# Two graph layers on one core: adjacency and mask of the graph two ahead are loaded at another place in the DMA queue

## The chip, the cores and the metric

The kernel runs on one core of a Trainium2 chip. The metric is the device time of one execution in microseconds, the median of the runs; a profiled execution of the same kernel gives the trace that is read here. The engines are named as the profile names them: PE is TensorE (PEld its weight loads), DVE is VectorE, ACT is ScalarE, POOL is GpSimd and SP is SyncE. In this kernel SyncE computes nothing: it issues nearly all DMA transfers, in the order of its program.

## The reference

64 graphs of 256 nodes with 512 features pass through two layers, in float32. Layer 0 is graph attention with 8 heads over the adjacency matrix; layer 1 is attention with 8 heads of 64 whose weights get two more terms, from the adjacency and from exp(-distance), where both the adjacency and the distance are the same matrix `adj`. Each layer ends with a residual and a layer norm. Cut to what matters:

```
# layer 0
feats = einsum('bnf,hfu->bhnu', X, W)
dense = leaky_relu(e_self[..., :, None] + e_neigh[..., None, :], 0.2)
dense = dense + NEG_BIG * (1.0 - A[:, None, :, :])
out = einsum('bhij,bhju->bhiu', softmax(dense), feats) + b
x = layernorm(x + relu(out))
# layer 1
q, k, v = split(x @ W_qkv)
attn = softmax(where(mask, q @ k.T * scale, -big)) * LA
attn = attn + LG * adj + LD * exp(-dist)          # dist is adj
x = layernorm(x + (attn @ v) @ W_out + b_out)
```

## The kernel before

One graph of 256 nodes is a block; a tile has 128 partitions, so a block has two row tiles. The work on a block is cut into stages: `turned` and `proj0` (features of layer 0, by Strassen-like products of halves), `attend0` (attention of layer 0), `proj1` (q, k and v of layer 1), `softmax1` and `attend1` (attention and output of layer 1). The main loop runs over the block number b from 2 to 63. Each pass is made of two functions written out by hand: `attention0_beside_projections1(b)` and then `attention1_beside_projections0(b)`. They interleave steps of several blocks: attention 0 of block b, projections of block b-1 for layer 1, features of block b+1, softmax of block b-1, output of block b-2 and the store of block b-4. `second_beside_first()` is the fill: it does the same for the first blocks, before the loop.

The order is that of the source. After each step, `in_order()` ties every new instruction to the one before it on the same engine, so that no scheduler moves it. What an engine does next is thus what the source names next for it, and a DMA that has to wait holds back all later DMAs of SyncE.

The order of SyncE's transfers in a pass, with their lines, is this. First half: the store of the output of block b-4 (`out_dram<-y`, L1216), the reload of rows for a residual (`y<-hs`, L1092), the rows of x for layer 0's residual of block b (`x<-in_x_dram`, `load_rows`, L147), the blocked x of block b+2 (`xb`, four DMAs, L123), the rows after layer 0 to memory and back in blocks (`hs<-x`, L899, and `hb<-hs`, four DMAs, L123). Second half: the maximum of the row factors (`gs<-top`, L586), the row factors to memory (`gs<-grow_sb`, four DMAs, L597) and back to all partitions (`gb<-gs`, 1,028 KB, L601); then the inverted sums of the softmax to memory (`rs<-rec`, L1038) and back to all partitions (`rb<-rs`, 1,024 KB, L1039); then the adjacency and the mask of block b+2 (`load_adj`, four DMAs of 64 KB, L123, and one of 32 KB, L143).

The buffers around them: `adj` has one buffer, which is read by one transposition on VectorE (`aT`, L739, shown as L130 in the trace) in the first half of each pass, before the load in its second half; `mask` has four; `y` has one, so `y<-hs` waits until the store before it has landed; the rows of x share one buffer with the blocks `hb`, which are transposed (`hT`) in the second half.

The readers that the text names: L823 (`attend0`, step `end`) adds the rows of x to layer 0's output on VectorE; L670 (`columns`) reads the broadcast row factors gb; L1059 (`attend1`, `weights`) reads the broadcast sums rb; L351 is VectorE's addition after a product, L790 the matmuls of layer 0's attention, L87 the matmuls of all projections.

Of the kernel before, what the change touches and what calls it, by code (L numbers as in the profile page):

```python
# [17 lines left out]
def kernel(  # L18
# [31 lines left out]
    NB, N, F = x.shape  # L50
# [43 lines left out]
    def in_order():  # L94

        new = []
        for ins in reversed(nc.cur_bb.bb.instructions):
            if ins.name in traced:
                break
            traced.add(ins.name)  # L100
            new.append(ins)
        for ins in reversed(new):
            if ins.engine in last:
                tc.add_manual_dep(
                    ins,
                    last[ins.engine],
                    mybir.DependencyInfo(
                        mybir.DependencyClass.NoSync, mybir.DependencyReason.DATA
                    ),
                    reason="order of the source",  # L110
                )
            last[ins.engine] = ins.name
# [7 lines left out]
    def load_blocks(dst, src):  # L120

        for q in range(Q):
            nc.sync.dma_start(  # L123
                dst[q * B : (q + 1) * B],
                src.rearrange("(k r) (c q s) -> q r c k s", r=B, q=Q, s=B)[q],
            )
# [7 lines left out]
    def load(b):  # L134

        XB[b] = io.tile([P, C, N // B, B], FT, tag="xb", name=f"xb_{b}", bufs=1)
        load_blocks(XB[b], x[b])

    def load_adj(b):
        ADJB[b] = io.tile([P, T, N // B, B], FT, tag="adj", name=f"adj_{b}", bufs=1)  # L140
        load_blocks(ADJB[b], adj[b])
        MROW[b] = io.tile([P, N], U8, tag="mask", name=f"mask_{b}", bufs=4)
        nc.sync.dma_start(MROW[b], nodemask[b].partition_broadcast(P))  # L143
# [105 lines left out]
    def load_rowmask():  # L249
        for g in range(NB // B):  # L250
            for k in range(Q):
                nc.sync.dma_start(
                    rowmask[k * B : (k + 1) * B, g].rearrange("p i b -> p (i b)"),
                    maskz[g * B : (g + 1) * B, :],
                )

    def load_wo():

        wo12 = work.tile([P, C2, F2], FT, tag="p", name="wo12", bufs=5)
        parts = w_out.rearrange("(k c p) (g f) -> k g p c f", k=2, p=P, g=2)  # L260
        for dst, k, g in ((wo_sb[0], 0, 0), (wo12, 0, 1), (wo_sb[1], 1, 0), (wo_sb[2], 1, 1)):
            nc.sync.dma_start(dst, parts[k, g])
        return wo12
# [976 lines left out]
    def do(stage, b, step, *args):  # L1240

        if 0 <= b < NB:
            if (stage, b) not in S:
                S[stage, b] = stages[stage](b)
            S[stage, b][step](*args)
            in_order()
# [133 lines left out]
    def second_beside_first():  # L1380


        b = 1
        for g in range(2):
            for t in range(T):
                do("attend0", b, "product", g, t)
        CW[0](3)
        do("attend0", b, "rec0", 0)
        do("attend0", b, "rec0", 1)
        do("proj1", 0, "qk", "p3")  # L1390
        load_rowmask()
        nc.sync.dma_start(bo_bc, b_out.partition_broadcast(P))
        WO["12"] = load_wo()
        do("turned", 2, "xT")
        do("proj1", 0, "qk_add", 12)
        do("turned", 2, "xC")
        do("attend0", b, "norm0", 0, 0)
        do("proj1", 0, "values", "p1")
        do("attend0", b, "norm0", 0, 1)
        do("attend0", b, "norm0", 1, 0)  # L1400
        do("proj1", 0, "values", "p2")
        do("proj1", 0, "v_add", 11)
        do("proj1", 0, "values", "p6")
        do("attend0", b, "norm0", 1, 1)
        do("attend0", b, "end")
        right_factors(wf_sb, wf12, (1, 2))
        do("proj1", 0, "values", "p5")
        do("proj1", 0, "values", "p7")
        do("proj1", 0, "v_add", 22)
        right_factors(wf_sb, wf12, (3,))  # L1410
        load(3)
        do("proj0", 2, "product", "p1")
        do("proj1", 0, "values", "p4")
        do("attend0", b, "squares", slice(0, 1), False)
        do("proj0", 2, "product", "p6")
        do("attend0", b, "squares", slice(1, 2), slice(0, 2))
        do("proj1", 0, "values", "p3")
        do("proj0", b, "shared")
        do("proj0", 2, "aT")
        do("proj1", 0, "v_add", 12)  # L1420
        do("proj0", 2, "product", "p5")
        do("proj0", 2, "product", "p7")
        do("attend0", b, "norm")
        do("proj1", b, "blocks")
        do("proj0", 2, "add", 22)
        do("proj0", 2, "product", "p2")
        do("proj0", 2, "product", "p4")
        do("proj0", 2, "far")
        do("proj0", 2, "product", "p3")
        right_factors(wo_sb, WO["12"], (0, 1))  # L1430
        do("proj0", 2, "add", 11)
        do("proj0", 2, "add", 12)
        do("proj0", 2, "rows")
        do("proj1", b, "from_rows", 0)
        do("proj1", b, "from_rows", 1)
        do("proj0", 2, "shared", 0)
        do("softmax1", 0, "scores", 0)
        do("proj0", 2, "shift")
        do("proj0", 2, "broadcast", 0)
        do("softmax1", 0, "scores", 1)  # L1440
        do("proj0", 2, "shared", 1)
        do("proj0", 2, "bias")
        do("proj0", 2, "broadcast", 1)
        do("proj0", 2, "shared", 2)
        do("proj1", b, "hC")
        do("softmax1", 0, "both", 0)
        do("softmax1", 0, "scores", 2)
        do("softmax1", 0, "both", 1)
        do("softmax1", 0, "scores", 3)
        do("softmax1", 0, "both", 2)  # L1450
        do("softmax1", 0, "both", 3)
        do("proj1", b, "qk", "p1")
        do("proj1", b, "qk", "p2")
        do("softmax1", 0, "sums")
        do("softmax1", 0, "invert")
        do("proj0", 2, "columns")
        do("softmax1", 0, "inverted")
        load_adj(3)

    def attention0_beside_projections1(b):  # L1460

# [83 lines left out]
    def attention1_beside_projections0(b):  # L1545


        do("attend1", b - 2, "values", 0)
        do("attend1", b - 2, "values", 1)
        do("proj0", b + 1, "rows")  # L1550
        do("proj0", b + 1, "shared", 0)
        do("attend1", b - 2, "values", 2)
        do("attend1", b - 2, "values", 3)
        do("softmax1", b - 1, "scores", 0)
        do("proj0", b + 1, "shared", 1)
        do("proj0", b + 1, "shift")
        do("proj0", b + 1, "shared", 2)
        do("proj0", b + 1, "broadcast", 0)
        if b + 2 < NB:
            do("turned", b + 2, "xT")  # L1560
        do("softmax1", b - 1, "scores", 1)
        do("attend1", b - 2, "half_blocks", 0)
        do("proj0", b + 1, "broadcast", 1)
        do("softmax1", b - 1, "both", 0)
        do("attend1", b - 2, "half_blocks", 1)
        do("softmax1", b - 1, "scores", 2, 0)
        do("softmax1", b - 1, "scores", 2, 2)
        do("softmax1", b - 1, "both", 1)
        do("softmax1", b - 1, "scores", 3, 0)
        do("attend1", b - 2, "product", "p1")  # L1570
        do("softmax1", b - 1, "scores", 2, 3)
        do("softmax1", b - 1, "scores", 3, 1)
        do("softmax1", b - 1, "both", 2)
        do("proj1", b, "hT")
        do("softmax1", b - 1, "both", 3)
        do("attend1", b - 2, "product", "p2")
        do("attend1", b - 2, "product_add", 11)
        do("attend1", b - 2, "product", "p6")
        do("attend1", b - 2, "product", "p5")
        do("attend1", b - 2, "product", "p7")  # L1580
        do("attend1", b - 2, "product_add", 22)
        do("softmax1", b - 1, "sums")
        do("proj1", b, "hC", (0,))
        do("softmax1", b - 1, "invert", 0)
        do("proj1", b, "hC", (2,))
        do("softmax1", b - 1, "invert", 1)
        do("proj1", b, "hC", (1,))
        do("softmax1", b - 1, "invert", 2)
        do("proj1", b, "hC", (3,))
        do("attend1", b - 2, "product", "p4")  # L1590
        do("proj0", b + 1, "bias")
        do("softmax1", b - 1, "inverted")
        if b + 2 < NB:
            load_adj(b + 2)
        do("attend1", b - 2, "product", "p3")
        do("attend1", b - 2, "product_add", 12)

# [126 lines left out]
```

## Time and profile before

| | us |
|---|---|
| median of 3 runs | 2842.19 (2837.35 to 2842.84) |
| the profiled execution | 2837.97 |
| its span, first to last instruction | 2835.8 |
| TensorE busy | 2791.4 (98%) |
| VectorE busy | 2561.0 (90%) |
| ScalarE busy | 1797.0 (63%) |
| DMA queue of SyncE, share of 16 DMA engines | 46.9% |

The granted TensorE clock was 0.998. TensorE is busy in nearly every slice of the span, so the time is read from the gaps: for a stall of TensorE, who released it, and for that one, what it had waited for. The longest waits of all engines stand at the top of the list of waits, but most belong to engines with time to spare:

```profile
POOL rstd_l L402 <- ACT junk L391: 1010.8, 129, 17.6
POOL nmean_l L385 <- DVE x L823: 996.1, 64, 28.0
```

In such a line the engine, its instruction and the releaser are followed by the total in microseconds, the number of waits and the longest. GpSimd is 15% busy, and its waits are idle time. The lines of the order of time begin with the start and the length in microseconds; SyncE's lengths are those of the issue, not of the transfer, and "x4" stands for four instructions in a row.

### The profile page before, as it was taken

Reading aid. Unit: us, or ns where it says so; the run is one execution under the profiler, and the core shown is the slowest. Engines: PE = TensorE matmul, PEld = TensorE weight load, DVE = VectorE, ACT = ScalarE, POOL = GpSimd, SP = SyncE. Lnnn points to the kernel's source line nnn. Section 1 sums busy time; section 2 is a strip of 40 time slices with the busy share of each in tenths; the row PEclk is TensorE's granted clock in tenths of the full one; section 3 lists DMA queues with packets and bytes.
Section 4 is the critical chain, followed back from the end, with each engine's and each line's share of the span. In section 5 each row is a group of like instructions: output and inputs, shape, how many; then the busy total and the mean of one; then the engine's idle time right before and its main releaser. Section 6 shows DMA issues by size and latency. Waiting matters only on the chain.

```text
span 2835.8 us, 93561 instructions
## 1 busy us (share of the span) xinstructions
PE 2791.4 (98%) x38584; PEld 2240.6 (79%) x38584; DVE 2561.0 (90%) x5264; ACT 1797.0 (63%) x5051; POOL 426.6 (15%) x1031
## 2 busy tenths in 40 slices
PE   9999999999999999999999999999999999999998
PEld 7778778788788787877777878887777878878775
DVE  7899999999989899899999999999998989999884
ACT  4666666666666666666666666666666666666663
POOL 1111211111111111111111111111111111111111
PEclk9999999999999999999999999999999999999999
DMA  6444544444454445444444454454544444444432
GB/s 140 117 114 134 133 126 137 127 131 141 118 137 136 111 138 135 125 137 118 129 137 124 135 138 120 137 131 124 143 118 129 129 125 137 131 130 138 118 118 72
DMA packets 778390, 362.58 MB, mean 128 GB/s; under 512 B 694767, under 2 KB 696303, under 8 KB 761966
## 3 DMA queue, kind: packets, MB, share of 16 engines
q1 hardware_dynamic: 775854, 356.07, 46.9%
q8 instruction: 306, 5.01, 0.7%
q14 instruction: 118, 0.97, 0.1%
q10 hardware_dynamic: 2112, 0.52, 0.1%
HBM read 288.11 MB, written 68.13 MB: 126 GB/s over the span
## 4 chain that ended last, share of the span: by engine, by line
PE 90%; DVE 4%; DMA 3%; ACT 2%; issue 1%; POOL 0%; SPq 0%; DVEq 0%; POOLq 0%
PE pq_p L87 26%; PE po_p L87 14%; PE pf_p L87 12%; PE pv_p L87 12%; PE pz L951 8%; PE av L1078 8%; PE av L790 7%; PE pd L988 2%; DMA x<-in_x_dram 1%; DMA out_dram<-y 1%; ACT v L725 1%; DVE p L1059 1%; DVE y L1097 1%; DVE p L1068 1%; PE po L87 0%
## 5 line engine op out<-in xcount | busy, mean ns | idle before, releaser
L87 PE MATMUL pq_p<-hC,wqk_sb 128*64 128x128 f32 x8192 | 474.3, 273 | 11.1 <-issue 9.5
L87 PEld LDWEIGHTS pq_p<-hC,wqk_sb 128*64 128x64 f32 x8192 | 450.5, 137 | 14.8 <-issue 12.0
L767 DVE SCALAR_TENSOR_TENSOR pT<-gb,ccol,at 128x256 f32<-128x256 f32 x992 | 403.0, 477 | 17.2 <-ACT ccol L677 17.2
L87 PE MATMUL pq_p<-hT,wqk_sb 128*64 128x128 f32 x6144 | 360.3, 273 | 0.6 <-issue 0.5
L972 ACT ACTIVATE p<-pz,hide 128x512 f32<-128x512 f32 x638 | 337.6, 619 | 30.4 <-PE pz L951 30.4
L87 PEld LDWEIGHTS pq_p<-hT,wqk_sb 128*64 128x64 f32 x6144 | 343.9, 137 | 11.1 <-issue 2.2
L1059 DVE TENSOR_TENSOR p<-p,rb 128x1024 f32<-128x1024 f32 x252 | 298.8, 1206 | 3.7 <-DMA rb<-rs 3.7
L1068 DVE TENSOR_TENSOR p<-p,ct 128x1024 f32<-128x1024 f32 x252 | 299.3, 1208 | 0.2
L811 ACT ACTIVATE x<-av,rec 128x64 f32<-128x64 f32 x1024 | 223.9, 334 | 62.2 <-DVE rec L803 62.2
L790 PE MATMUL av<-v,pT 128*64 128x65 f32 x8192 | 253.5, 222 | 5.6 <-issue 4.9
L87 PE MATMUL pf_p<-wf_sb,xC 128*64 128x264 f32 x1984 | 257.4, 387 | 1.1
L87 PE MATMUL pv_p<-wv_sb,hC 128*64 128x256 f32 x2048 | 247.2, 380 | 11.0 <-DVE v L351 8.6
L348 ACT COPY qk<-pq_p 128x512 f32<-128x512 f32 x256 | 148.8, 581 | 171.2 <-PE pq_p L87 168.2
L790 PEld LDWEIGHTS av<-v,pT 128*64 128x64 f32 x8192 | 249.5, 138 | 8.0 <-issue 6.8
L725 ACT ACTIVATE v<-v 128x64 f32<-128x64 f32 x1024 | 251.2, 336 | 3.8 <-DVE v L716 3.7
L348 ACT COPY v<-pv_p 128x256 f32<-128x256 f32 x256 | 95.4, 373 | 226.6 <-PE pv_p L87 226.5
L951 PE MATMUL pz<-qk 64*128 64x256 f32 x2048 | 238.7, 383 | 0.0
L87 PE MATMUL po_p<-wo_sb,oC 128*64 128x256 f32 x1984 | 237.6, 381 | 0.5
L1078 PE MATMUL av<-p,v 128*64 128x256 f32 x2016 | 230.1, 379 | 2.1 <-DVE p L1068 2.1
L402 POOL TENSOR_SCALAR rstd_l<-rstd_l 128x2 f32<-128x2 f32 (+1 forms) x130 | 76.5, 589 | 1010.9 <-ACT junk L391 1010.8
L951 PEld LDWEIGHTS pz<-qk 64*128 64x128 f32 x2048 | 192.5, 187 | 44.8 <-issue 24.8
L87 PEld LDWEIGHTS pv_p<-wv_sb,hC 128*64 128x64 f32 x2048 | 162.3, 137 | 73.9 <-DVE v L351 13.3
(175 smaller groups left out, 4631.1 us busy)
## 6 DMA issues: line engine op xcount, KB each, us to landing
rb<-rs SPq DMA_DIRECT2D x63, 1024.0 KB
gb<-gs SPq DMA_DIRECT2D x62, 1028.0 KB
hs<-x SPq DMA_DIRECT2D x64, 512.0 KB
xb<-in_x_dram SPq DMA_DIRECT2D x252, 128.0 KB
x<-in_x_dram SPq DMA_DIRECT2D x63, 512.0 KB
y<-hs SPq DMA_DIRECT2D x63, 512.0 KB
out_dram<-y SPq DMA_DIRECT2D x63, 512.0 KB
hb<-hs SPq DMA_DIRECT2D x248, 128.0 KB
```

The lines of the kernel that those rows point to most:

```text
L87: matmul(dst[cols], lhsT[:, cols], rhs, **flags)
L348: nc.scalar.copy(out[COPIES[p]], dst)
L402: nc.gpsimd.tensor_scalar(rstd, rstd, 1.0 / F, EPS, op0=ALU.mult, op1=ALU.add)
L725: nc.scalar.activation(v[:, :U], v[:, :U], AF.Copy, scale=v[:, U : U + 1])
L767: nc.vector.scalar_tensor_tensor(pT[h][:, j, :], GB[b][h], CCOL[b][:, j, h : h + 1], AT[b][:, j, :], op0=ALU.max, op1=ALU.mult,)
L790: matmul(av[r * half : (r + 1) * half, k, :], pT[h][:, j, i : i + half], V0[b][:, j, h, :UA], start=(j == 0), stop=(j == T - 1),)
L811: nc.scalar.activation(X1[b][:, t, h * U : (h + 1) * U], av[:, k, :U], AF.Copy, scale=REC0[g][:, t, k : k + 1],)
L951: matmul(pz[r][:, j, :], QK[b][rows, g, 1, j * P : (j + 1) * P], QK[b][rows, g, 0, :], start=True, stop=True,)
L972: nc.scalar.activation(to, of, AF.Exp, bias=hide[:, j, b : b + 1], scale=U**-0.5)
L1059: nc.vector.tensor_mul(p, p, REC[b][:, k : k + 2, g // 2, :] .unsqueeze(2) .to_broadcast([P, 2, T, N]),)
L1068: nc.vector.tensor_add(p, p, CT[b].unsqueeze(1).to_broadcast([P, 2, T, N]))
L1078: matmul(av[0][r * U : (r + 1) * U, g % 2, :], V1[b][:, j, 2 * g + r, :], PROBS[b][g][:, r, j, :], start=(j == 0), stop=(j == T - 1),)
```

## The change

`load_adj(b + 2)` is called at another place of the same function: right behind the step that issues the broadcast of the row factors (gb), and no longer behind the step that issues the broadcast of the inverted sums (rb). In the fill, `load_adj(3)` is called right behind the transposition that reads the only `adj` buffer (`aT` of block 2), and no longer at the end of the function. `load_adj` itself and all other steps stay as they are.

```
@@ in second_beside_first
         do("proj0", b, "shared")
         do("proj0", 2, "aT")
+        load_adj(3)
         do("proj1", 0, "v_add", 12)
...
         do("softmax1", 0, "inverted")
-        load_adj(3)
@@ in attention1_beside_projections0
         do("attend1", b - 2, "half_blocks", 0)
         do("proj0", b + 1, "broadcast", 1)
+        if b + 2 < NB:
+            load_adj(b + 2)
         do("softmax1", b - 1, "both", 0)
...
         do("softmax1", b - 1, "inverted")
-        if b + 2 < NB:
-            load_adj(b + 2)
         do("attend1", b - 2, "product", "p3")
```

In the program as built, the order of the instructions of TensorE, VectorE, ScalarE and GpSimd is the same before and after; on SyncE's queue the five DMAs of `load_adj` stand ahead of `rs<-rec` instead of behind `rb<-rs`, and in the fill ahead of `hs<-x` of block 1.

More of the change, by code (lines that the diff above doesn't have):

```diff
@@ L1419, in second_beside_first @@
         do("proj0", 2, "aT")
+        load_adj(3)
         do("proj1", 0, "v_add", 12)
@@ L1457, in second_beside_first @@
         do("softmax1", 0, "inverted")
-        load_adj(3)
     def attention0_beside_projections1(b):
@@ L1563, in attention1_beside_projections0 @@
         do("proj0", b + 1, "broadcast", 1)
+        if b + 2 < NB:
+            load_adj(b + 2)
         do("softmax1", b - 1, "both", 0)
@@ L1592, in attention1_beside_projections0 @@
         do("softmax1", b - 1, "inverted")
-        if b + 2 < NB:
-            load_adj(b + 2)
         do("attend1", b - 2, "product", "p3")
```

## The prediction

> **What bounds the kernel now.** I read the page first, then the waits of TensorE, VectorE and SyncE's queue, then the order of time on SyncE in one bad block and in the last block.
>
> ```profile
> PE 2791.4 (98%) x38584; PEld 2240.6 (79%) x38584; DVE 2561.0 (90%) x5264; ACT 1797.0 (63%) x5051; POOL 426.6 (15%) x1031
> ...
> q8 instruction: 306, 5.01, 0.7%
> ```
>
> TensorE is busy for 98% of the span, so a change of DMA order can only win what TensorE stands still. The loop shows how much that is. The broadcast of the sums (rb<-rs, L1039) is issued once a block, at 131.66 us for the first full block and at 2736.54 us for the last: 60 blocks of 43.41 us. Blocks without a stall repeat every 42.66 us or so. So 60 x 0.75 = 45 us are stalls; that is the whole stake, plus little in the fill. What are they?
>
> ```profile
> PE pq_p L87 <- issue: 10.0, 10, 2.0
> PE pv_p L87 <- DVE v L351: 8.6, 10, 1.8
> PE av L790 <- issue: 4.9, 4, 2.4
> ```
>
> Two kinds (columns: total us, times, longest). First, TensorE waits for v, which VectorE adds late because it stood before L823, the residual of layer 0, for rows of x:
>
> ```profile
> DVE x L823 <- DMA x<-in_x_dram: 21.1, 16, 3.9
> ...
> DVE x L823 <- issue: 16.6, 17, 2.7
> ```
>
> (12.9 us more are booked under ACT, 8 times; all are the same instruction, and I read them all as the x load.) Second, "issue": TensorE waits for nothing that the program asked for. In every one of these the last packet of queue q8 (16,384 bytes, TensorE's instructions) began 2.2 to 2.4 us before TensorE went on. So these are late instruction fetches.
>
> A bad block on SyncE, then the instruction on VectorE that pays:
>
> ```profile
> 1162.93 0.35 SPq L601 DMA_DIRECT2D gb<-gs  x1
> 1170.05 0.56 SPq L1038 DMA_DIRECT2D rs<-rec  x1
> 1171.78 0.35 SPq L1039 DMA_DIRECT2D rb<-rs  x1
> 1172.18 2.83 SPq L123 DMA_DIRECT2D adj<-in_adj_dram  x4
> 1175.05 1.90 SPq L143 DMA_DIRECT2D mask<-in_nodemask_dram  x1
> 1177.05 0.39 SPq L1216 DMA_DIRECT2D out_dram<-y  x1
> 1182.64 0.37 SPq L1092 DMA_DIRECT2D y<-hs  x1
> 1183.05 0.47 SPq L147 DMA_DIRECT2D x<-in_x_dram  x1
> ```
>
> ```profile
> 1189.76 0.69 DVE L823 SCALAR_TENSOR_TENSOR x<-x,x 128x512 f32<-128x512 f32 x1 [3.87 <-DMA x<-in_x_dram]
> ```
>
> Adjacency and mask keep SyncE for 4.8 us ahead of the store; y<-hs cannot be issued before the store has landed, and x stands behind it. The last block loads no adjacency anywhere:
>
> ```profile
> 2736.54 0.35 SPq L1039 DMA_DIRECT2D rb<-rs  x1
> 2740.14 0.39 SPq L1216 DMA_DIRECT2D out_dram<-y  x1
> 2743.44 0.38 SPq L1092 DMA_DIRECT2D y<-hs  x1
> 2743.86 0.47 SPq L147 DMA_DIRECT2D x<-in_x_dram  x1
> ```
>
> Counted from rb, the store goes out at 3.60, where it waits for ScalarE's normalisation and no longer for SyncE; x goes out at 7.3, against 9 to 12.4 in the others. Its packets end at 12.6, and L823 starts at 14.0 without a wait. And where adjacency is to go, SyncE idles:
>
> ```profile
> SPq L1038 <- DVE nd L670: 418.5, 60, 7.3
> SPq L1092 <- DMA out_dram<-y: 224.1, 61, 5.2
> ```
>
> Behind gb it waits 418.5 / 60 = 7.0 us for rec before rs<-rec.
>
> [...] the 128-byte packets of adjacency begin at 1175, just as the 8,192-byte packets of rb run out, and the store's 2,048-byte packets follow at 1178. [...] 5.01 MB / 306 = 16.4 KB, and 78,401 TensorE records / 306 = 256. [...]
>
> **The change part by part.** Nothing is added: the loop moves five DMAs a block (4 x 64 KB and 32 KB) on SyncE's queue from behind rb to behind gb. TensorE, VectorE, ScalarE and GpSimd keep their order. The moved DMAs pass rs<-rec and rb<-rs, nothing else. Their buffers are free: adj was read by the transposition (L739) in the first half of the same block, and there are four masks.
>
> The new place. gb is issued 8.8 us before rb (6.8 to 9.1). Four issues at 0.63 to 0.8 us are 2.8 us. The mask's issue took 1.9 us more [...], and ended 4.3 to 7.6 us after rb's issue, typically 4.8; gb is as large as rb, so I take 4.8 behind gb: done at -4.0, and rs<-rec goes at -1.73. The packets: gb moved from 1164 to 1168, the DMA engines then idled until 1171.6. Adjacency's 2,048 packets of 13 ns are 1.7 us over 16 engines, 2.2 us as seen; it would end at about -1.4, the mask's few packets at -1. rs<-rec may be held up to 0.5 us by them. I take 0.2. The store has 3.2 us of slack on SyncE behind rb, and rb's reader (L1059 at +8.9) over 3 us after the landing: nothing.
>
> The old place, x rows. The store goes out at 3.6 instead of 4.4 to 7.7; x moves by at least 1.2 us, most where it was latest. How a wait at L823 counts: 3.87 us made a block of 45.50, 2.19 of 43.82, 0.98 of 43.10, under 0.5 of 42.7. So roughly the first microsecond is hidden by TensorE's lead. Over the blocks whose stall is this one, the excess over 42.67 sums to 23 us. I shifted each block's landing by what its store is late of 3.6, plus 0.5 us for adjacency's packets ahead of it: one wait stays above 1 us (the block at 1171, 1.7 us). Removed: 21 of 23. If cover is lacking elsewhere (slow landing), the same waits come back at most as before.
>
> The old place, instruction fetch. Twelve blocks with an "issue" stall carry 21 us over 42.67. The fetches fell due 3.9 to 6.3 us after rb, were served at 7.4 to 11.5, behind rb, adjacency and store in turn, and TensorE's densest stretch (the av products, 70 instructions a microsecond at +5 to +9) ran dry. Without adjacency the store's packets end at about 6.7 instead of 8.5 to 9. A fetch due at 4.2 is needed by about 6.3; served at 6.6, it costs 0.3 instead of 2.4. From below: nothing is gained, as the y and x loads (7.5 to 12.5) now block instead. From above: 19. I take 12.
>
> The new place, fetch. Transfers now fill -7.8 to -1 without a gap. A fetch due at -8 is served by -1.4, its instructions are needed at about +0.7, less 2.3 us of latency: up to 0.4 us late. One block in six has a fetch due in the critical 2 us. Bounds 0 and 10 us; I take 2.
>
> The fill. The one load moved waits for the transposition at 71.4 and is issued from 71.5 to 74.6; hs<-x at 73.20 goes 1.5 us later, with no reader for blocks; gs<-top (76.57) and gb (82.14) keep their times. Behind rb at 91 the av products lose their 6.3 us (3.3 in the loop) to a late fetch; some of it goes. Bounds 0 and 4; I take 2.
>
> Sum: 21 + 12 - 2 + 2 = 33. The profiled execution took 2837.97 us (span 2835.8 and 2.2 around it), so 2805. The median of the runs is 4.2 us higher; I take that for more stalls of the same two kinds, half of which would go: 2807.
>
> **The rivals.** (1) Fetch stalls only move: x waits go, but the fetches find the y and x loads or gb with adjacency. For: the packets of y and x start 2 us earlier, into the dense stretch; the last block, without adjacency, still shows a fetch due at 7.3 served at 9.9. Against: after +9 TensorE needs 40, then 18 instructions a microsecond, so such fetches have time. 2842 - 21 = 2821. (2) x does not come earlier: the store is held by ScalarE (SyncE waited for it 56 times, 28.8 us) and by its landing behind rb. Against: the last block. Then 2842, no change. (3) Slower: adjacency's issues hold SyncE behind gb until after rec is ready. rs, rb, store, y and x all follow in one queue. It decides where rb comes over 1.3 us later than now, as x then lands later than before; the mask's issue would have to take 8.5 us instead of 4.8. At 2.5 us every block's x is 1.2 us later than today, about 1.1 us a block beyond the hidden part: 66 - 23 - 12 = 31 slower, 2873. For: the mask's issue did take 7.6 us in one block, and gb is only 5 us ahead of rs in two. Against: 7.0 us of idle SyncE in 60 blocks.
>
> **How the numbers follow.** Forecast 0.62 (2796 to 2815 for itself), rival 1 0.20 (2815 to 2834), rival 2 0.07, rival 3 0.11. About 0.2%, 5.7 us, is what a measurement of this kernel tells from no change. Faster: 0.62 + 0.20, less a little of rival 1's edge, 0.81; within 0.2%: 0.08; slower: 0.11. The range 2796 to 2836 leaves out rivals 2 and 3.
>
> **What would show it.** Right: x issued 7.3 to 8 us after rb; the L823 waits at 50 us in all fall under 15; TensorE's "issue" waits under 8 us; the SyncE wait at L1038 falls to 2 us. Wrong: rb's distance from gb grows beyond 9 us; TensorE's "issue" waits keep 16 us or turn up around rb's issue; L1216 is not held by ScalarE.

## The result

The changed kernel takes 2797.98 us (median of 4 runs, 2796.61 to 2799.13) against 2839.81 us (2837.35 to 2842.84; median of 4, one run more than in the table of before): a ratio of 0.9852, with a 95% interval of 0.9835 to 0.9869. That is 41.8 us less. The profiled execution took 2798.83 us, 39.1 us less than the one before, with a span of 2796.9 us. The forecast was 2807 us. The direction held, and so did the two terms that it was made of; the profiled gain was almost 20% larger than forecast (39 us against 33), and one of the terms was much too small.

The page of the changed kernel, the line of engine busy times:

```profile
PE 2778.1 (99%) x38584; PEld 2201.3 (79%) x38584; DVE 2561.5 (92%) x5264; ACT 1794.7 (64%) x5051; POOL 417.0 (15%) x1031
```

The 38,584 matmuls are the same, and still TensorE's busy time is 13 us shorter than the 2791.4 us before. The granted clock is 0.998 in both. Of the 39 us, 26 are idle time that went and 13 are busy time that went, so a part of the stalls must have been booked as busy: a busy share of 98% hid more standing than 2%.

TensorE's waits of the changed kernel, from the list of waits (total us, times, longest):

```profile
PE pv_p L87 <- ACT v L348: 3.4, 3, 2.4
PE av L1078 <- DVE p L1068: 2.1, 2, 1.6
PE pq_p L87 <- ACT qk L348: 1.5, 3, 0.7
PE av L790 <- issue: 1.1, 4, 0.4
```

Both kinds of stall are nearly gone. "Issue" was 16.3 us in three groups before (10.0 and 4.9, and 1.4 under pv_p) and is now 1.4 (this line and 0.3 under pq_p); the wait of pv_p for VectorE's v, 8.6 us before, is no longer in the list. The first line was there before with the same 3.4 us.

The reason on VectorE, what ended the idle time ahead of L823 in the changed kernel:

```profile
  ACT v L348: 1.9, 1
  ACT x L811: 0.8, 2
  DMA x<-in_x_dram: 0.8, 2
  issue: 0.4, 1
```

That is 3.9 us in 6 waits, against 51.4 us in 43 before (21.1, 16.6, 12.9 and 0.8). On SyncE, one block in order of time, near the place of the bad block of before:

```profile
1147.81 0.35 SPq L601 DMA_DIRECT2D gb<-gs  x1
1148.21 2.62 SPq L123 DMA_DIRECT2D adj<-in_adj_dram  x4
1150.87 2.80 SPq L143 DMA_DIRECT2D mask<-in_nodemask_dram  x1
1154.99 0.55 SPq L1038 DMA_DIRECT2D rs<-rec  x1
1156.71 0.31 SPq L1039 DMA_DIRECT2D rb<-rs  x1
1160.32 0.39 SPq L1216 DMA_DIRECT2D out_dram<-y  x1
1163.16 0.37 SPq L1092 DMA_DIRECT2D y<-hs  x1
1163.58 1.23 SPq L147 DMA_DIRECT2D x<-in_x_dram  x1
```

Adjacency and mask now fill SyncE's wait for rec, and rs<-rec is still issued 7.2 us behind gb. The store goes out 3.61 us behind rb (5.27 in the block of before) and x 6.87 us behind it (11.27). SyncE's waits of the changed kernel say it for all blocks, and below them stands the line of before that the prediction only quotes:

```profile
SPq L1216 <- ACT v L725: 202.8, 60, 3.5
...
SPq L1092 <- DMA out_dram<-y: 187.4, 61, 5.3
...
SPq L1038 <- DVE nd L670: 106.1, 60, 6.2
```

```profile
SPq L1216 <- ACT v L725: 28.8, 56, 3.5
```

SyncE waits for rec 1.8 us a block instead of 7.0, and for ScalarE's normalisation ahead of the store 3.4 us instead of 0.5. The list names L725, but what ends there is the normalisation of y just ahead of it on ScalarE; in the block above:

```profile
1158.78 1.52 ACT L410 ACTIVATE y<-y,shift_l,rstd_l 128x512 f32<-128x512 f32 x2
```

It ends at 1160.30 us, and the store is issued at 1160.32. ScalarE, no longer SyncE, sets when the store goes. From rb of the first full block (130.56 us) to that of the last (2696.10) are now 60 blocks of 42.76 us, 0.65 us less each, 39 us in all: the whole gain lies in the loop. 42.69 us is the most frequent distance, so about 4 us of stalls are left there.

That distance is also the most frequent one before, so each block's excess over it can be put down to its stall (a block with both kinds is counted under "issue"). Before, 14 blocks with an issue stall carry 24 us and 26 others with a wait at L823 carry 19.5 us. In the changed kernel 5 blocks carry 2.6 us and one carries 0.9.

### The profile page after: what moved, and what is told of

It is laid out like the page before. It is cut to its first block, busy times and chain, and to the rows that moved or that the text cites. A ratio compares the mean times of both kernels' runs of the same rounds, so it can differ in the third digit from the quotient of the medians.

```text
span 2796.9 us, 93442 instructions
## 1 busy us (share of the span) xinstructions
PE 2778.1 (99%) x38584; PEld 2201.3 (79%) x38584; DVE 2561.5 (92%) x5264; ACT 1794.7 (64%) x5051; POOL 417.0 (15%) x1031
## 4 chain that ended last, share of the span: by engine, by line
PE 97%; DVE 1%; ACT 1%; DMA 0%; issue 0%; POOL 0%; SPq 0%; DVEq 0%; POOLq 0%
PE pq_p L87 27%; PE po_p L87 14%; PE pf_p L87 13%; PE pv_p L87 13%; PE av L790 9%; PE pz L951 8%; PE av L1078 8%; PE pd L988 2%; PE po L87 1%; PE pf L87 0%; DVE p L1059 0%; DMA gb<-gs 0%; DVE p L1068 0%; PE pg L663 0%; ACT x L811 0%
## 5 line engine op out<-in xcount | busy, mean ns | idle before, releaser
L1059 DVE TENSOR_TENSOR p<-p,rb 128x1024 f32<-128x1024 f32 x252 | 299.0, 1207 | 3.9 <-DMA rb<-rs 3.9
L725 ACT ACTIVATE v<-v 128x64 f32<-128x64 f32 x1024 | 251.2, 336 | 3.8 <-DVE v L716 3.7
L402 POOL TENSOR_SCALAR rstd_l<-rstd_l 128x2 f32<-128x2 f32 (+1 forms) x130 | 95.0, 731 | 1054.9 <-ACT junk L391 1054.8
L980 DVE SCALAR_TENSOR_TENSOR both<-p 128x512 f32<-128x512 f32 x256 | 172.9, 677 | 41.5 <-ACT p L972 41.3
```

What stands on the lines that cost most here:

```text
L725: nc.scalar.activation(v[:, :U], v[:, :U], AF.Copy, scale=v[:, U : U + 1])
L980: nc.vector.scalar_tensor_tensor(both[g], p[:, :, 0, :], TINY, p[:, :, 1, :], op0=ALU.add, op1=ALU.add)
L1059: nc.vector.tensor_mul(p, p, REC[b][:, k : k + 2, g // 2, :] .unsqueeze(2) .to_broadcast([P, 2, T, N]),)
```

## The experiments

Times are compared by the ratio to the kernel before, run beside them on the same chip, since that kernel's median moved between 2835.9 and 2839.8 us. "Waits at L823" and TensorE's "issue" waits are totals in the profiled execution. The first runs ask whether there are two causes, each with its own price, and where the harm sits.

Some texts tell when an instruction fetch was due and when it was served. Served means that its packet on queue q8 begins. Due is TensorE's place in each block of 256 of its records (78,401 records to 306 packets) from which on the earliest fetches of these traces were seen to begin, about 150 records into the block; the lateness is the time between the two. These figures, and the medians of many blocks, are worked out from the traces' single records, which no view prints.

**e1_fill_only.** The fill of the change alone:

```
         do("proj0", 2, "aT")
+        load_adj(3)
         do("proj1", 0, "v_add", 12)
...
         do("softmax1", 0, "inverted")
-        load_adj(3)
```

> Only the fill's load is moved; the loop is as before. In the trace of the changed kernel the first full block starts 1.1 us earlier than before and the rest of the gain lies in the loop. Theory (the gain is the loop's): 2838 to 2840 us against 2839.8 before. Rival (the fill sets a better rhythm for the instruction fetches of the whole loop): 2830 or less.

Measured: 2837.77 us against 2835.91, ratio 1.0002 (0.9989 to 1.0016). Waits at L823 54.5 us, issue waits 16.9 us: the loop is as it was. The fill is worth nothing that can be measured (the interval would hide some 3 us), and sets no rhythm for the loop.

**e3_x_early.** Adjacency stays in the old place, and the rows of x move to the gap behind gb instead, as soon as their buffer has been read (`hT`):

```
         do("attend1", b - 3, "rows_again")
-        load_rows(b)
+        if b == 2:
+            load_rows(b)
...
         do("proj1", b, "hT")
+        if b + 1 < NB:
+            load_rows(b + 1)
```

> Adjacency and mask stay behind rb, in the loop and in the fill; instead the rows of x are loaded behind gb, ahead of rs<-rec. It takes away the late x and leaves adjacency between rb and the store. Theory of two terms (late x 23 us, late instruction fetches 19 us, each by itself): about 2817, waits at L823 under 5 us in all, TensorE's issue waits still about 16 us. Rival A (all of the gain is the earlier x; the fetches are only late where x is): about 2800. Rival B (all of the gain is the fetches): about 2840.

Measured: 2818.44 us, ratio 0.9938 (0.9923 to 0.9954), 17 us less. VectorE's only wait left at L823 and TensorE's first waits in this run:

```profile
DVE x L823 <- ACT x L811: 0.8, 2, 0.4
```

```profile
PE av L790 <- issue: 9.8, 5, 2.7
PE pq_p L87 <- issue: 7.1, 6, 1.9
```

x is never late, and the late fetches stand as before (17.3 us with 0.4 under pv_p). The forecast of the two terms was 2817. Both rivals with one cause fall.

**e4_adj_behind_store.** The other half alone: nothing between rb and the store, but adjacency ahead of y and x:

```
         do("attend1", b - 4, "store")
+        if 2 < b < NB - 1:
+            load_adj(b + 1)
         do("attend1", b - 3, "rows_again")
```

(Without the call behind `inverted` in the loop.)

> Adjacency and mask are loaded between the store and y<-hs: nothing stands between rb and the store, but y and x are issued as late as before or later (about 9 us behind rb). Theory of two terms: the fetches' 19 us go and the x waits stay, 2815 to 2830, TensorE's issue waits under 3 us, L823 waits 30 us or more in all. Rival A (only x counts): 2840 or more. Rival B (only the fetches count): about 2800.

Measured: 2810.33 us, ratio 0.9908 (0.9892 to 0.9925), 26 us less, 5 us below the range expected. VectorE's waits, then TensorE's:

```profile
DVE x L823 <- DMA x<-in_x_dram: 21.0, 22, 2.7
...
DVE x L823 <- issue: 18.8, 24, 2.8
```

```profile
PE pv_p L87 <- issue: 1.9, 1, 1.9
...
PE av L790 <- issue: 1.5, 4, 0.8
```

Issue waits fall to 3.4 us, just over the 3 expected, and the waits at L823 stay, 45.6 us of them. But they cost less than such a sum did before, as they are many and short (2.8 us at the longest against 3.9): by the excess over 42.69 us, 33 blocks with such a wait and no issue stall carry 6 us, where 26 carried 19.5. So e4 took more than the fetches, which can account for the 5 us below its range. e3 shows the term of x by itself; e4 shows that the fetches are a second term, but mixes in a part of the first. That the two gains (17 and 26 us) add up to that of the change is therefore in part chance.

**e6_adj_only** and **e5_mask_only.** The change's two halves: the four adjacency DMAs alone behind gb, or the mask alone. `load_adj` is split, and in e6:

```
         do("proj0", b + 1, "broadcast", 1)
+        if b + 2 < NB:
+            load_adj_only(b + 2)
...
         do("softmax1", b - 1, "inverted")
         if b + 2 < NB:
-            load_adj(b + 2)
+            load_mask(b + 2)
```

In e5 the two names change places.

> Only the four adjacency DMAs move behind gb; the mask (32 KB, whose issue took 1.7 us at the median and 3.1 at most) stays behind rb. Theory (what counts is adjacency's packets and issues ahead of the store): 2798 to 2806. Rival C (what counts is that SyncE is held by an issue [...], which the mask alone would suffer as well): the store still goes out at 4.5 or later behind rb, and 2815 or more.

> Only the mask moves behind gb; the four adjacency DMAs stay behind rb, whose issues end about 3.2 us behind it, before ScalarE lets the store go at 3.6. Theory (adjacency's packets, [...], do the harm): store issued at 3.6, but y still 8 to 9 us behind rb, TensorE's issue waits 10 us or more: 2818 to 2830. Rival C (SyncE's issue time does it): all of the gain, about 2798.

Measured: e6 2797.15 us, ratio 0.9863 (0.9848 to 0.9878), all of the gain, as the theory had it (1 us below its range). e5 2807.34 us, ratio 0.9888 (0.9864 to 0.9913), 32 us less, where the theory said 2818 or more and issue waits of 10 us. TensorE's issue waits in e5 (line numbers are 7 higher, since the split adds lines):

```profile
PE av L797 <- issue: 2.9, 5, 1.1
```

So the theory fell in one point: adjacency's packets ahead of the store's do not by themselves make fetches late. Rival C was right about the fetches, but not about all of the gain: what e5 lacks of it lies in 21.9 us of waits for x, which is issued 8.6 us behind rb at the median, against 7.5 in the changed kernel. What changes with either half gone is how long the issue of the mask takes. Its line in before, in the changed kernel, in e5 and in e6 (issue time min/median/max in ns):

```profile
L143 SPq DMA_DIRECT2D mask<-in_nodemask_dram x64: 620/1704/3127, 10.7 to 2696.8; - x64
```

```profile
L143 SPq DMA_DIRECT2D mask<-in_nodemask_dram x64: 619/2620/3363, 11.0 to 2648.7; - x64
```

```profile
L150 SPq DMA_DIRECT2D mask<-in_nodemask_dram x64: 417/424/1781, 10.3 to 2655.5; - x64
```

```profile
L150 SPq DMA_DIRECT2D mask<-in_nodemask_dram x64: 411/424/1707, 10.6 to 2654.4; - x64
```

The mask is issued in 0.42 us without the adjacency just ahead of it, and takes 1.7 us behind rb and adjacency and 2.6 us behind gb and adjacency. Only the pair holds SyncE past the moment at which ScalarE frees the store; with either one gone the store goes out at 3.6 us behind rb (median of the loop, as in the changed kernel), not at 4.95.

**e10_adj_twice.** A second dose in the old place, on e3, where x cannot be late. The copied words are read by nobody, so the result is the same:

```
         if b + 2 < NB:
             load_adj(b + 2)
+            again = dram.tile([N * N // B, 2, B], FT, tag="again", ...)
+            rows = N * N // B // Q
+            for q in range(Q):
+                nc.sync.dma_start(
+                    again[q * rows : (q + 1) * rows, 0],
+                    adj[b + 2].rearrange("n (c s) -> (n c) s", s=B)[q * rows : (q + 1) * rows],
+                )
```

> e3_x_early with a dose more: behind adjacency and mask the same 256 KB are copied once more in 128-byte pieces, from memory to memory into a scratch that nobody reads, ahead of the store. x is early and can't be late. Theory (a fetch due 4 to 6 us behind rb waits for adjacency's and the store's packets): each of some 12 late fetches gets 2 us or more later and others join them, issue waits of 40 us or more instead of 17, and 2840 to 2865 us. Rival F (those fetches are late for another reason, such as rb alone): issue waits 17 us as in e3_x_early and about 2818.

Measured: 2810.57 us, ratio 0.9900 (0.9876 to 0.9924). TensorE's issue waits:

```profile
PE av L790 <- issue: 4.3, 4, 1.5
...
PE pq_p L87 <- issue: 2.8, 5, 0.9
```

More bytes ahead of the store made the fetches less late: 7.1 us of stalls against 17.3 in e3. Theory and rival both fall. The trace shows what differs: the store now goes out 8.1 us behind rb (4.9 in e3), so that its 2,048-byte packets come after 9 us, when TensorE's densest stretch (5 to 9 us) is over, and the stretch itself lies beside 128-byte packets. The fetches that fell due at 3.8 to 5.2 us were served at 5.2 to 7.8 us here, and at 5.6 to 9.0 in e3. The packets of the mask lie where they lay in e3, so they alone are not what makes fetches late. Not all of this run is understood: its blocks with late fetches carry 10 us of excess, and others 8 us more.

**e11_x_and_mask_early.** The new theory's own test: e3 plus the mask of e5 (x and mask behind gb), so that adjacency alone stands between rb and the store.

> The rows of x and the mask behind gb; the four adjacency DMAs stay between rb and the store. Theory after the first runs (adjacency ahead of the store does harm to the fetches only together with the mask, which sends the store out 1.3 us later and its packets to where the fetches fall due): issue waits 2 to 4 us as in e5_mask_only, no x waits, 2796 to 2802. Rival G (adjacency alone still costs the fetches, and e5_mask_only hid it behind its x waits): issue waits 8 us or more, 2806 to 2812.

Measured: 2800.39 us, ratio 0.9863 (0.9847 to 0.9880). TensorE's issue waits:

```profile
PE av L797 <- issue: 1.8, 4, 0.6
...
PE pq_p L87 <- issue: 0.9, 3, 0.5
```

Against e3, 18 us less by the medians and 21 by the ratios (the chips differ), for moving 32 KB of mask. The runs fit one account: what makes fetches late is the time at which the store's packets lie. Behind adjacency and mask they run at 6 to 9 us (6.2 to 8.8 at the median before), and a fetch that falls due at 4 to 5 us, and is 1.7 us late at the median even in the changed kernel, meets them. With the store issued at 3.6 us they are mostly over by 7 here, and by 6 in the changed kernel (97% of them had begun by then). A store delayed by something other than these loads was not run.

**e9_x_and_adj_early.** The changed kernel, and e3's edit on top: everything into the gap behind gb.

> As changed, and the rows of x behind gb as well: gb, adjacency, mask and x, 1.8 MB, in the 7 us behind gb. Theory: x cannot be late and nothing lies behind rb but the store, so 2793 to 2799, unless rs<-rec or the sums' broadcast is held back by more than 3 us. Rival E (the place behind gb is full): rs lands 2 us later or more, rb's reader L1059 waits for DMA, and fetches due 8 us ahead of rb are late: 2805 or more.

Measured: 2809.52 us, ratio 0.9894 (0.9865 to 0.9923), about 12 us slower than the change alone. SyncE's wait for the landing of rs in the changed kernel and here, then TensorE's issue waits here:

```profile
SPq L1039 <- DMA rs<-rec: 76.0, 63, 2.0
```

```profile
SPq L1039 <- DMA rs<-rec: 144.8, 63, 3.3
```

```profile
PE av L790 <- issue: 9.1, 11, 1.6
...
PE pq_p L87 <- issue: 2.1, 3, 1.2
```

The gap is full: SyncE waits 2.3 us a block for rs to land, where it waited 1.2. The sums' broadcast goes out 9.9 us behind gb instead of 9.0, and its packets and the store's move back with it, towards the densest stretch of TensorE. The stalls belong to fetches that fell due 0.9 to 3.0 us behind rb; they were served at 4.8 to 6.0, while in the changed kernel fetches due at that time were served at 3.5 to 4.7. Rival E was right that the place is full and in its time, but not in its signs: the broadcast came 1 us later and not 2, its reader L1059 waited as little as before (4.6 us against 3.9), and the late fetches were not those ahead of rb.

**e7_adj_behind_x** and **e8_x_early_adj_late.** Two other places for adjacency and mask: behind the rows of x (`load_adj(b + 1)` right after `load_rows(b)`, the fill as before), or, with x behind gb as in e3, right after `rows_again`.

> The smallest other way: adjacency and mask stand behind the load of the rows of x, in the first half of the next pass; the fill is as before. Theory (any place not between rb and the store will do): x issued 7 to 8 us behind rb as in the changed kernel, issue waits under 4 us, 2795 to 2801. Rival D (only the gap behind gb is free): adjacency's packets at 12 to 15 us hold back fetches or the blocked x, 2805 or more.

> The rows of x are loaded behind gb as in e3_x_early, and adjacency and mask behind y<-hs; the fill is the changed kernel's. Theory: any place will do that is not between rb and the store, and both terms go: 2793 to 2800. Rival D (adjacency must lie in the gap behind gb): adjacency's packets at 8 to 11 us hold back the fetches that fall due at 6 to 9 us, 2805 or more.

Measured: e7 2798.23 us, ratio 0.9854 (0.9837 to 0.9871); e8 2795.65 us, ratio 0.9848 (0.9824 to 0.9872). The gap behind gb is not needed: behind the load of x, or behind y<-hs with x already loaded, adjacency and mask do as little harm. Between the store and y<-hs they still hold x back (e4).

**e12_changed_again** and **e13_x_early_adj_late_again.** The changed kernel and e8 on one chip, to see whether e8 is better.

> The changed kernel once more, beside the next run on the same chip. 2796 to 2800, as it was.

> e8_x_early_adj_late once more (x behind gb, adjacency and mask behind y<-hs), for a comparison on the same chip. Theory (it also removes the few x waits that the changed kernel keeps, 3.9 us in 6 waits): 1 to 3 us less than the changed kernel. Rival: no difference, within 0.5 us.

Measured: 2796.48 us (2794.56 to 2797.05) and 2796.20 us (2794.72 to 2799.14). No difference that these runs can tell. In e13 the waits at L823 are 0.8 us, and its 60 blocks take only 2 us more than 60 times 42.69 us; the few stalls that the change left are too small to show in a measurement.

## Why the prediction was right, and where its sizes were off

- **The late x**: forecast 21 of 23 us, and right but for a little. Waits at L823 fell from 51.4 to 3.9 us, x was issued 7.5 us behind rb at the median (forecast 7.3 to 8), and the blocks with such waits and no issue stall went from 19.5 us of excess to 0.9. e3 took this term alone and gained 17 us. The last block, which loads no adjacency, had been a sound model of the new loop: the store at 3.60, as now.
- **The late fetches in the old place**: forecast 12 of 21 us, with rival 1 (they only move) at a chance of 0.20. This is the term that was mis-sized. Issue waits fell from 16.3 to 1.4 us, and the blocks with such stalls from 24 us of excess to 2.6: 21 us gained. The estimate for one fetch was close (0.3 us of stall): the stalls that are left in the changed kernel, 0.2 to 0.4 us each, come from fetches due at 3.4 to 4.2 us and served at 6.2 to 6.6. The hedge against the y and x loads, which took the term down from 19, was not needed: fetches that fell due at 6 to 9 us were served as late as 12 us behind rb without a stall. TensorE begins 70 to 74 instructions a microsecond at 5 to 8 us, some 36 at 9 to 12 and about 20 from then on. The cause was also told too simply: by these runs it is the pair of adjacency and mask that puts the store where it hurts (e5, e6, e11), not the bytes ahead of it (e10).
- **The new place**: forecast a loss of 2 us, from fetches held until gb and adjacency had passed at -1.4 us. No stall was seen. The fetches due at -8.3 to -7.3 us were served at -3.7 to -2.9, while adjacency's packets ran (-4.5 to -2.1 at the median of the loop). They did not wait for all of these. Fetches due at -6.7 to -6.1 us were held by them: 3.9 us late at the median, against 2.6 before. TensorE did not need them so soon.
- **SyncE behind gb**: forecast that the mask's issue ends 4.8 us behind gb; in the block shown it ended at 5.9 us, as its issue took 2.8 us. The slack of 7 us covered it, and SyncE's wait at L1038 fell to 1.8 us (forecast 2). Rival 3 needed SyncE to be held until after rec was ready. That did not come even with 512 KB more (e9): rs<-rec still went out 7.2 us behind gb, and the 12 us were lost by its later landing. (The 7.6 us that rival 3 quotes is when the mask's issue ended behind rb; no issue of the mask took over 3.1 us.)
- **The fill**: forecast 2 us. The trace has the first full block 1.1 us earlier, but that is within the scatter of the traces: 130.8 to 131.7 us with the old fill, 130.6 to 132.5 with the new. e1 shows no gain, and e6 and e7 keep the old fill and are as fast as the change.
- **The sum**: 33 us forecast for the profiled execution, 39 measured. The fetch term gave 9 us more than forecast, and the loss of 2 us did not come; the x term gave about 2 us less, and the fill's 2 us were not seen. The stake was a little smaller than the 45 us forecast, 43.5, since blocks without a stall repeat every 42.69 us and not 42.66.

## What to carry to other kernels

In a kernel that is 98% busy on one engine, look at the stalls by their causes: here both led back to one place in a DMA queue, where a load with half a pass to spare stood ahead of a store that others had to wait for. Order such a queue by when the result is needed, put loads with slack into the queue's own waits, and measure how much a wait can hold before it is filled (e9). And count instruction fetches among the users of the DMA engines: a stall in which the engine waits for nothing the program asked for may be cured by moving a transfer, as 16.3 us of them here became 1.4.

## What the runs showed of the hardware

- The time that SyncE took to issue the mask (32 KB) went with what stood ahead of it in the queue: at the median 0.42 us without adjacency just ahead (e5, e6), and behind adjacency's four DMAs of 512 packets each 1.7 us (before, with rb ahead of them), 2.6 (the changed kernel, gb ahead) or 0.8 (e8, y<-hs ahead). Why, these runs do not show.
- How late the fetches of TensorE's instructions were served went with the transfers beside them. Fetches due 0.5 to 3.1 us behind rb were late by 2.9 us at the median before, when rb's 8,192-byte packets ran (they began at 1.0 to 4.3 us and took 0.32 us each). Fetches due 3.5 to 5.2 us behind rb were late by 3.3 us at the median before and 3.0 in e3, with the store's 2,048-byte packets ahead; by 2.4 in e10, with 128-byte packets in their place; and by 1.7 in the changed kernel, with the store's packets over sooner. Fetches due 6.1 to 6.7 us ahead of rb were late by 2.6 us before, by 3.9 with adjacency's 256 KB behind gb and by 4.7 with the 512 KB of x there (e3). Whether the size of the packets or the number of bytes counts, these runs do not tell apart.
- Every stall of TensorE of over 0.25 us that was booked under "issue", in all the traces, ended 2.1 to 2.8 us after the beginning of a fetch's packet.
- With the stalls went most of the spread. The 33 runs of before lie between 2829.57 and 2846.65 us, the 8 of the changed kernel between 2794.56 and 2799.13. On one chip, 7 runs of before span 11.4 us and 4 of the changed kernel 2.5. That the stalls are the spread is likely, but was not tried by itself.
